# The opening turns of a two-layer graph kernel: loads, weight sums and the first attention in another order

## The chip, the cores and the metric

One core of a Trainium2 chip runs the kernel as a single program. The metric is the device time of one execution in microseconds (us), lower is better; the times given are medians of several executions on the chip. The profile is of one execution more, recorded by the hardware profiler. Its engines are PE (TensorE, matrix products), DVE (VectorE), ACT (ScalarE), POOL (GpSimd) and SP (SyncE, which issues the DMAs here).

## The reference

Two layers are computed on x, 128 graphs of 64 nodes with 768 features. The second layer is ordinary masked attention and is not touched. The first is this, cut to what matters (W has 12 heads of 64 features):

```python
h = jnp.einsum('bnd,ade->bane', feat_in, W)
th = jnp.tanh(h)
attn_src = jnp.einsum('bane,aeo->bano', th, w_src)
attn_dst = jnp.einsum('bane,aeo->bano', th, w_dst)
attn = attn_src + jnp.swapaxes(attn_dst, 2, 3)
attn = jnp.where(attn >= 0, attn, LEAKY_ALPHA * attn)
attn = jnp.where(~adj[:, None, :, :], jnp.float32(-999.0), attn)
attn = jax.nn.softmax(attn, axis=-1)
feat_out = jnp.einsum('banm,bame->bane', attn, h) + b
feat_out = jax.nn.elu(feat_out)          # heads side by side
gate = jax.nn.sigmoid(feat_in @ H_w.T + H_b)
return gate * feat_out + (1.0 - gate) * feat_in
```

Around each layer stand a residual and a layer norm: `x = _layernorm(x + layer(x))`. The second layer begins with v, q and k, products of that x with three more 768 x 768 weights.

## The kernel before

The 8192 rows are cut into 64 tiles of 128 rows (two graphs each), and two tiles make a pair: 32 pairs (`NP`). The first layer's loop (L851) takes a turn for each pair, and one more turn for what is left over.

**Products.** Each 256 x 768 times 768 x 768 product is split into 2 x 2 blocks and done with seven block products instead of eight (Winograd's variant of Strassen's scheme). That needs sums of the blocks of both operands. `block_sums` (L165) makes four sums of x's blocks, and `weight_sums` (L146) four of a weight's blocks, in place:

```python
lambda: eng.tensor_tensor(w[:, T1], w[:, T3], w[:, B11], ALU.subtract),
lambda: eng.tensor_tensor(w[:, T2], w[:, B22], w[:, T1], ALU.subtract),
lambda: eng.tensor_tensor(w[:, T4], w[:, B21], w[:, T2], ALU.subtract),
lambda: eng.tensor_tensor(w[:, T3], w[:, B22], w[:, T3], ALU.subtract),
```

The block of the weight that is loaded as T3 is the upper right one. The seven block products have numbers; number i reads the weight block `OF_B[i]`: 1 reads B11, 2 B21, 3 B22, 4 T4, 5 T1, 6 T2, 7 T3. Products 1, 2, 3 and 4 read x's own blocks or its fourth sum, 5, 6 and 7 its first three sums. A `Job` (L181) is one such product: h (features of all heads, weight w0), g (gate, weight hw) and v (values of the second layer, weight wv). Products 6, 7 and 4 add onto the bank that 1 left. `way_out` (L212) brings a bank out: h on ACT (`S.copy`) for first blocks and on DVE for additions, g wholly on DVE, v like h. `step` (L238) issues a block product and then the way out of the product before it.

**Order.** All instructions are placed by hand (`manual_schedule`): each engine runs its own in the order in which the code issues them, and waits where an input isn't there. `TURN` (L65) lists the 21 products of a turn: "h1" is product 1 of the new pair's h, "g" its gate, "v" the old pair's values, "u" what was left of v's products of the pair before. After the product at position `pos`, everything that `at(pos, ...)` has put into the plan (L871 on) is issued. While the new pair p gets its h and g, the old pair q = p - 1 gets its attention. In the first turn there is no old pair and no v, so the list shrinks to the 14 products of h and g.

**The attention of a tile** goes through these steps, in order: `products` (L633, tanh on ACT, product with the w_dst and w_src rows on DVE and POOL), `terms` (L642, the sums `sd` on DVE, their write to DRAM `dstd` and the read back `dd`), `with_bias` (L659, POOL adds b to h, two DMAs make the half-swapped copy `hx`), `logits` (L671, DVE), `leaky` (L683, ACT), `masked` (L687, DVE), `exps` (L700, ACT, `prob`), `probs_by_nodes` (L718, PE transposes, ACT copies to `pT`), `attend` (L729, 24 small PE products), `features` (L745, DVE, then exp on ACT), `residual` (L763, POOL), `elu1` and `gated` (L768, L773, DVE), `stats` and `normed` (the layer norm), `by_features` (L791, PE transposes of x1, ACT copies to `x1T`), and `v_begins`, which lets v's products start. `mask` (L806) loads a pair's adjacency and makes `nadj` of it on DVE. Tile t1 of a pair comes first, t0 after.

**Opening.** Before the loop (L541 to L557) SP issues, in this order: x transposed of pair 0 (768 KB), four blocks of w0 (576 KB each), four of hw, the two rows of wsd, hb, b0, four blocks of wv. The sums of x are made on POOL, w0's on DVE, then hw's on POOL, then b0 + 1 and wv's four sums on DVE. Only then does the loop begin, so on DVE all of these stand ahead of the first ways out.

Of the kernel before, what the change touches and what calls it, by code (L numbers as in the profile page):

```python
# [49 lines left out]

LAST = [
    "u4", "u3", "q1", "q2", "k1", "k2", "q6", "q5", "q7", "Q1", "q4", "Q2", "q3", "k6", "k5", "k7",
# [10 lines left out]
    "h1", "h2", "u4", "u3", "h6", "g1", "h5", "h7", "g2", "g6", "h4",  # L66
    "h3", "g5", "g7", "v1", "v2", "g4", "v6", "g3", "v5", "v7",
]


@with_exitstack
def kernel(
# [58 lines left out]
        nc.sync.dma_start(out=t, in_=src.rearrange("(f p) -> p f", p=P))  # L131
        return t

    def load_weight(src, tag, name):

        w = wpool.tile([P, 7, HK, HALF], F32, tag=tag, name=name)
        for block in (B11, B21, B22, T3):
            load_block(src, w, block)
        return w

# [5 lines left out]
    def weight_sums(eng, w):  # L146

        return [
# [6 lines that stand above are left out]
    def all_of(steps):  # L155
        for s in steps:
            s()
# [351 lines left out]
    with ExitStack() as ph, ExitStack() as ph_r:  # L509
# [3 lines left out]
        def load_rows(pool, src, n, name):  # L513
            t = pool.tile([P, n], F32, name=name, bufs=1)
            nc.sync.dma_start(out=t, in_=src.partition_broadcast(P))
            return t

        def load_xT(p):
            t = sbr.tile([P, KC, PAIR * P], F32, tag="xT", name=f"xT_{p}")
            nc.sync.dma_start(out=t, in_=xT[p])  # L520
            return t

        def load_x(p):
            ts = []
# [16 lines left out]
        xTs = {0: load_xT(0)}  # L541

        w0_w = weights["q"] = load_weight(w0, "wa", "w0_wq")
        hw_w = weights["k"] = load_weight(hwT, "wb", "hw_wk")
        wsd = sbr.tile([P, 2, D], F32, name="wsd", bufs=1)
        nc.sync.dma_start(out=wsd[:, 0, :], in_=wdst.partition_broadcast(P))
        nc.sync.dma_start(out=wsd[:, 1, :], in_=wsrc.partition_broadcast(P))
        hb_bc = load_rows(sbr, hb, D, "hb_bc")
        b01_bc = load_rows(sb, b0, E0, "b01_bc")
        A = {}  # L550
# [37 lines left out]
        def h_job(p):  # L588
            def at(m, n):
                return h_of(p, m)[:, n * J0 : (n + 1) * J0, :E0]  # L590

            def as_heads(b):
                return b.rearrange("p (j e) -> p j e", e=E0)

            return token_job(
                f"h{p}",
                A[p],
                w0_w,
                lambda mn, b: S.copy(at(*mn), as_heads(b)),
                lambda mn, b: V.tensor_tensor(at(*mn), as_heads(b), at(*mn), ALU.add),  # L600
                lambda b: S.copy(at(1, 0), as_heads(b)),
            )
# [201 lines left out]
            nc.sync.dma_start(out=x1T_d[p], in_=x1Ts[p])  # L804

        def mask(p):  # L806
            ad = load_adj(sb, 2 * p, PAIR, f"adj_{p}")
# [25 lines left out]
            B[q], v_sums[q] = sums_of(V, sb, "sv", x1Ts[q], f"v{q}")  # L833

        def x_sums(p):
            A[p], steps = sums_of(G, sbr, "sx", xTs[p], f"x{p}")
            all_of(steps)

        row_sums = []

# [6 lines left out]
            jobs["q"], jobs["k"] = feature_jobs(0, 0)  # L847
            jobs["Q"], jobs["K"] = feature_jobs(0, 1)

        v_sums = {}  # L850
        for p in range(NP + 1):  # L851
            q = p - 1
            new, old = p < NP, 0 <= q < NP
            t0, t1, n0, n1 = 2 * q, 2 * q + 1, 2 * p, 2 * p + 1
            if new:
                jobs["h"], jobs["g"] = h_job(p), gate_job(p)
            plan = {}

            def at(pos, ok, *acts):
                if ok:  # L860
                    plan.setdefault(pos if new else LAST_AT.get(pos, pos), []).extend(acts)
# [10 lines left out]
            at(1, old, do(residual, t1))  # L872
            at(2, old, do(attend, t1), do(gate_tanh, t0))
            at(3, old, do(features, t1), do(probs_by_nodes, t0), do(residual, t0))
            at(4, old, do(elu1, t1), do(gated, t1))
            at(5, old, do(attend, t0), do(stats, t1))
            at(6, old, do(features, t0), do(normed, t1))
            at(7, old, do(elu1, t0), do(gated, t0))
            at(8, old, do(by_features, t1), do(stats, t0))
            at(9, old, do(normed, t0))  # L880
            at(12, old, do(v_begins))
            at(15, old, lambda: v_sums[q][0](), lambda: v_sums[q][1](), do(spill_features, q))
            at(16, old, lambda: v_sums[q][2]())
            at(19, old, lambda: v_sums[q][3]())

            at(0, p + 1 < NP, lambda: xTs.__setitem__(p + 1, load_xT(p + 1)))
# [4 lines left out]
            at(11, old, do(by_features, t0))  # L891
# [6 lines left out]
            at(17, p + 1 < NP, do(x_sums, p + 1))  # L898
# [21 lines left out]
            for pos, (job, i) in enumerate(TURN if new else LAST):  # L920
                ok = {"h": new, "g": new, "v": old, "u": 0 <= p - 2 < NP}.get(job, True)
                if ok:
                    step(jobs[job], int(i))
                else:
                    flush()
# [115 lines left out]
```

## Time and profile before

| | us |
|---|---|
| median of 3 runs | 2976.0 (2974.97 to 2976.16) |
| the profiled execution | 2976.17 |
| its span in the profile | 2974.4 |
| PE busy | 2921.3 |
| DVE, ACT, POOL busy | 1819.8, 1006.3, 821.0 |

The span runs from the first to the last recorded instruction. In a row of the timeline the columns are the start, the duration, the engine, the line of the kernel, the operation, what it writes and reads (buffer numbers left out), how many records are merged, and in brackets the idle time of that engine before it with what ended it. A block product of h, g or v appears as six matmul records. The granted clock of PE (PEclk) is 1.00 at full speed.

The time of PE by stretch of the opening (busy us of 7.60, 21.06 and so on; further columns left out here):

| stretch, us | PE busy | DVE busy | POOL busy | PEclk |
|---|---|---|---|---|
| 0 to 8.88 | 0.00 | 0.15 | 2.18 | 1.00 |
| 8.88 to 16.48 | 6.10 | 2.83 | 2.41 | 1.00 |
| 16.48 to 37.54 | 9.91 | 9.76 | 10.52 | 0.82 |
| 37.54 to 64.13 | 19.00 | 14.42 | 11.97 | 0.82 |
| 64.13 to 79.56 | 11.85 | 11.53 | 3.69 | 0.78 |
| 79.56 to 142.94 | 63.38 | 49.66 | 20.60 | 1.00 |

### The profile page before, as it was taken

What the parts mean: (1) busy time and instruction counts of PE and PEld (TensorE: products, weight loads), DVE (VectorE), ACT (ScalarE), POOL (GpSimd) and SP (SyncE); (2) the same over time, 40 slices, a digit from 0 to 9 for tenths busy, and PEclk for the clock granted to TensorE, in tenths of its full rate; (3) what the DMA queues carried; (4) which work ended last, traced back from release to release, by engine and by line L of the source; (5) the groups of instructions that cost most, each with busy time, mean ns of one, the idle gap of its engine ahead of it and who ended that gap; (6) DMA issues with size and microseconds to landing.
All of it is one profiled execution on the core that took longest, in us unless ns stands there. A gap on an engine that the chain in (4) does not pass through costs nothing.

```text
span 2974.4 us, 45312 instructions
## 1 busy us (share of the span) xinstructions
PE 2921.3 (98%) x18048; PEld 2021.3 (68%) x18048; DVE 1819.8 (61%) x3013; ACT 1006.3 (34%) x1761; POOL 821.0 (28%) x654
## 2 busy tenths in 40 slices
PE   5999999999999999999989999999999999999999
PEld 3666666666666666666578777787777887777875
DVE  4888888888888888888844334433443443443345
ACT  2444444443444444434422222222222222222221
POOL 4333333243233333433422211212111212121121
PEclk8999999999999999999999999999999999999999
DMA  5334333333333333333523211222112222112221
GB/s 171 100 111 128 102 118 117 114 108 110 119 120 102 118 126 105 110 113 121 175 88 92 69 58 57 86 86 76 63 54 67 86 76 72 58 56 83 87 80 48
DMA packets 179537, 284.81 MB, mean 96 GB/s; under 512 B 46720, under 2 KB 113280, under 8 KB 179328
## 3 DMA queue, kind: packets, MB, share of 16 engines
q1 hardware_dynamic: 179328, 281.93, 29.1%
q8 instruction: 143, 2.34, 0.3%
q14 instruction: 66, 0.54, 0.1%
HBM read 167.81 MB, written 101.06 MB: 90 GB/s over the span
## 4 chain that ended last, share of the span: by engine, by line
PE 95%; DVE 2%; DMA 2%; SPq 1%; ACT 0%; issue 0%; POOL 0%; POOLq 0%; DVEq 0%; ACTq 0%
PE y_o L203 8%; PE y_k L203 8%; PE y_h L203 8%; PE y_v L203 8%; PE y_g L203 8%; PE y_q L203 8%; PE z_h L203 4%; PE z_v L203 4%; PE z_o L203 4%; PE z_k L203 4%; PE z_q L203 4%; PE z_g L203 4%; PE x_o L203 2%; PE x_k L203 2%; PE x_v L203 2%; PE x_g L203 2%
## 5 line engine op out<-in xcount | busy, mean ns | idle before, releaser
L766 POOL TENSOR_TENSOR x<-gate,x 128x768 f32<-128x768 f32 x64 | 117.2, 1831 | 315.3 <-ACT gate L817 315.3
L438 POOL TENSOR_TENSOR y<-y,bf_bc 128x768 f32<-128x768 f32 x64 | 115.8, 1839 | 308.7 <-DMA y<-x1d 308.7
L462 DVE TENSOR_TENSOR y<-y_o,y 128x384 f32<-128x384 f32 x128 | 71.3, 557 | 202.2 <-PE y_o L203 199.4
L320 DVE TENSOR_TENSOR kT<-z_k,kT 128x256 f32<-128x256 f32 x96 | 40.7, 424 | 238.6 <-PE z_k L203 135.3
L639 POOL TENSOR_TENSOR th<-th,wsd 128x768 f32<-128x768 f32 x64 | 116.3, 1817 | 159.5 <-DVE th L638 159.5
L255 POOL TENSOR_TENSOR rs_b<-ve_b,minus_half 128x1 f32<-128x1 f32 x64 | 35.2, 549 | 453.2 <-DVE ve_b L253 451.3
L173 POOL TENSOR_TENSOR sq_q<-a,a 128x768 f32<-128x768 f32 x16 | 29.7, 1855 | 432.8 <-PE y_o L203 315.9
L203 PE MATMUL y_g<-hw_wk,sx_x 128*128 128x384 f32 x384 | 136.5, 492 | 11.1 <-DVE gate L615 11.1
L203 PE MATMUL y_h<-w_wq,xT 128*128 128x384 f32 x384 | 137.4, 495 | 8.9 <-DMA w_wq<-in_w_dram 8.9
L203 PE MATMUL y_k<-a,hw_wk 128*128 128x256 f32 x576 | 144.6, 387 | 0.0
L203 PE MATMUL y_q<-a,w_wq 128*128 128x256 f32 x576 | 140.2, 379 | 1.5 <-ACT qT L319 1.5
L203 PE MATMUL y_q<-sq_q,w_wq 128*128 128x256 f32 x576 | 140.3, 380 | 1.4 <-ACT qT L319 1.2
L203 PE MATMUL y_k<-sq_q,hw_wk 128*128 128x256 f32 x576 | 140.1, 379 | 1.4 <-ACT kT L319 1.4
L255 POOL TENSOR_TENSOR rs_a<-ve_a,minus_half 128x1 f32<-128x1 f32 x64 | 35.3, 552 | 382.6 <-DVE ve_a L253 382.6
L203 PE MATMUL z_q<-sq_q,w_wq 128*128 128x256 f32 x576 | 140.1, 379 | 0.0
L203 PE MATMUL z_k<-sq_q,hw_wk 128*128 128x256 f32 x576 | 140.0, 379 | 0.0
L203 PE MATMUL z_v<-wv,sv_v 128*128 128x384 f32 x384 | 137.5, 494 | 1.6 <-DVE v L629 1.6
L319 ACT ACTIVATE qT<-y_q,bq_c 128x256 f32<-128x256 f32 x144 | 67.4, 469 | 211.8 <-PE y_q L203 211.8
L203 PE MATMUL y_v<-wv,sv_v 128*128 128x384 f32 x384 | 136.6, 492 | 1.5 <-DVE sv_v L174 1.5
L367 ACT ACTIVATE sc<-sc 128x512 f32<-128x512 f32 x48 | 30.2, 630 | 318.5 <-DVE sc L366 318.5
L203 PE MATMUL z_h<-w_wq,sx_x 128*128 128x384 f32 x384 | 137.5, 494 | 0.0
L203 PE MATMUL y_h<-w_wq,sx_x 128*128 128x384 f32 x384 | 136.0, 491 | 1.5 <-DVE w_wq L150 1.5
(167 smaller groups left out, 6807.5 us busy)
## 6 DMA issues: line engine op xcount, KB each, us to landing
xT<-in_xT_dram SPq DMA_DIRECT2D x32, 768.0 KB, 6.7
x<-in_x_dram SPq DMA_DIRECT2D x64, 384.0 KB, 3.6
dd<-dstd SPq DMA_DIRECT2D x128, 192.0 KB, 3.4
x1d<-x SPq DMA_DIRECT2D x64, 384.0 KB, 2.5
x1Td<-x1T SPq DMA_DIRECT2D x32, 768.0 KB, 4.8
vd<-v SPq DMA_DIRECT2D x64, 384.0 KB, 2.9
a<-x1Td SPq DMA_DIRECT2D x64, 384.0 KB, 3.6
v<-vd SPq DMA_DIRECT2D x384, 64.0 KB, 2.3
```

The lines of the kernel that those rows point to most:

```text
L173: lambda: e.tensor_tensor(s1, a21, a22, ALU.add),
L203: T.matmul(to[:, : self.n], lhsT, rhs, start=kc == 0 and not more, stop=kc == HK - 1, skip_group_check=more,)
L255: G.tensor_tensor(rstd, ve, minus_half, ALU.pow)
L319: lambda mn, bk_: S.activation(at(*mn), bk_, AF.Identity, bias=bias(mn[1])),
L320: lambda mn, bk_: V.tensor_tensor(at(*mn), bk_, at(*mn), ALU.add),
L367: S.activation(sc, sc, AF.Exp, scale=SCALE)
L438: G.tensor_tensor(y, y, pools["bf"], ALU.add)
L462: V.tensor_tensor(at(*mn), b, at(*mn), ALU.add)
L639: G.tensor_tensor(th[:, 1, :], th[:, 1, :], wsd[:, 1, :], ALU.mult)
L766: G.tensor_tensor(xp, st[t]["gate"], xp, ALU.mult)
```

## The change

The first three turns get lists and places of their own, and the rest of the loop keeps `TURN`.

- **Loads.** x transposed of pair 0 comes in two halves, each ahead of the w0 blocks that need it; w0's T3 ahead of its B22; hb and b0 ahead of hw; hw in the order B11, B21, T3, B22; wsd after hw; wv's blocks are issued inside the first turn, after pair 0's x.
- **Weight sums.** w0's on DVE in the order T1, T2, T3, T4. hw's on DVE (POOL before), one each after positions 6 to 9 of the first turn. wv's on DVE after positions 4, 5, 7 and 8 of the second turn. b0 + 1 after position 7 of the first.
- **First turn** (`FIRST`, 13 products): h mostly ahead of the gate; g4 goes into the second turn as "G4". Pair 1's sums of x come at position 12.
- **Second turn** (`SECOND`, 22 products): pair 1's h and g, G4, then "H1" (the next pair's h1), v1, v2, v6, v5, v7 of pair 0 and "H2". The new pair's steps and the old pair's steps have separate tables of places, so that pair 0's attention begins at position 6 or later. Steps placed past the end of a list are carried into the next turn.
- **Third turn**: `TURN` without its first two products, and all steps two positions earlier.
- **All turns**: the adjacency's load stays at position 3, `nadj` on DVE moves from position 3 to 6.

```diff
+FIRST = ["h1", "h2", "h5", "h6", "g1", "h7", "g2", "h4", "g6", "g5", "g7", "h3", "g3"]
+FIRST_AT = {3: 0, 6: 10, 8: 3, 11: 8, 12: 12, 13: 12, 14: 13, 15: 14, 16: 14, 17: 14, 18: 15, 19: 16, 20: 17}
+SECOND = [
+    "h1", "G4", "h2", "g1", "g2", "h6", "h5", "h7", "g6", "h4",
+    "g5", "g7", "h3", "g4", "g3", "H1", "v1", "v2", "v6", "v5", "v7", "H2",
+]
+SECOND_AT = {11: 10, 12: 13, 13: 13, 14: 14, 15: 14, 16: 15, 17: 16, 18: 18, 19: 19, 20: 20}
+SECOND_OLD = {
+    0: 7, 1: 7, 2: 8, 3: 9, 4: 10, 5: 11, 6: 12, 7: 12, 8: 13, 9: 14, 11: 15, 12: 15, 15: 16, 16: 17, 19: 19,
+}
+THIRD_AT = {pos: max(pos - 2, 0) for pos in range(len(TURN))}
+TURNS = {
+    0: (FIRST, FIRST_AT, {}),
+    1: (SECOND, SECOND_AT, SECOND_OLD),
+    2: (TURN[2:], THIRD_AT, THIRD_AT),
+}
...
-        w0_w = weights["q"] = load_weight(w0, "wa", "w0_wq")
-        hw_w = weights["k"] = load_weight(hwT, "wb", "hw_wk")
+        for kh, blocks in ((0, (B11,)), (1, (B21, T3, B22))):
+            rows = slice(kh * HK, (kh + 1) * HK)
+            nc.sync.dma_start(out=xTs[0][:, rows, :], in_=xT[0][:, rows, :])
+            for block in blocks:
+                load_block(w0, w0_w, block)
+        hb_bc = load_rows(sbr, hb, D, "hb_bc")
+        b01_bc = load_rows(sb, b0, E0, "b01_bc")
+        hw_w = weights["k"] = load_weight(hwT, "wb", "hw_wk", (B11, B21, T3, B22))
...
-        all_of(weight_sums(V, w0_w))
-        all_of(weight_sums(G, hw_w))
-        V.tensor_scalar(b01_bc, b01_bc, 1.0, None, ALU.add)
-        wv_w = load_weight(wv, "wc", "wv")
-        all_of(weight_sums(V, wv_w))
+        t1, t2, t4, t3 = weight_sums(V, w0_w)
+        all_of((t1, t2, t3, t4))
+        wv_w = wpool.tile([P, 7, HK, HALF], F32, tag="wc", name="wv")
...
-            at(0, old, do(probs_by_nodes, t1), do(exps, t0), do(gate_tanh, t1))
+            was(0, do(probs_by_nodes, t1))
+            at(0, old, do(exps, t0), do(gate_tanh, t1), places={0: 6} if p == 1 else of_old)
...
-            at(3, new, do(mask, p))
+            at(3, new, lambda: adjs.__setitem__(p, load_adj(sb, 2 * p, PAIR, f"adj_{p}")))
+            at(6, new, do(mask, p))
...
+            at(17, p + 1 < NP, do(x_sums, p + 1), places={17: 12} if p == 0 else of_new)
...
+            if p == 0:
+                for pos, act in zip((6, 7, 8, 9), weight_sums(V, hw_w)):
+                    at(pos, True, act, places={})
+                for block in (B11, B21, T3, B22):
+                    at(8, True, do(load_block, wv, wv_w, block))
+                at(7, True, lambda: V.tensor_scalar(b01_bc, b01_bc, 1.0, None, ALU.add))
+            if p == 1:
+                at(14, True, third_begins, places={})
+                for pos, act in zip((4, 5, 7, 8), weight_sums(V, wv_w)):
+                    at(pos, True, act, places={})
+            for pos, acts in carried.items():
+                plan[pos] = acts + plan.get(pos, [])
+            carried = {pos - len(turn): acts for pos, acts in plan.items() if pos >= len(turn)}
+            for pos, (job, i) in enumerate(turn):
+                step(jobs[job], int(i))
```

`third_begins` prepares H, pair 2's h, from the two of x's blocks that its products 1 and 2 read; its sums of x come in the third turn. `was` is `at` for the old pair's steps with their own table of places.

More of the change, by code (lines that the diff above doesn't have):

```diff
@@ L132, in load_cols, with load_weight @@
         return t
-    def load_weight(src, tag, name):
+    def load_weight(src, tag, name, order=(B11, B21, B22, T3)):
         w = wpool.tile([P, 7, HK, HALF], F32, tag=tag, name=name)
-        for block in (B11, B21, B22, T3):
+        for block in order:
             load_block(src, w, block)
@@ L520, in load_xT @@
             nc.sync.dma_start(out=t, in_=xT[p])
-            return t
+            xTs[p] = t
         def load_x(p):
@@ L539, in sums_of @@
             )
-        xTs = {0: load_xT(0)}
-        w0_w = weights["q"] = load_weight(w0, "wa", "w0_wq")
-        hw_w = weights["k"] = load_weight(hwT, "wb", "hw_wk")
+        xTs, A = {}, {}
+        xTs[0] = sbr.tile([P, KC, PAIR * P], F32, tag="xT", name="xT_0")
+        w0_w = weights["q"] = wpool.tile([P, 7, HK, HALF], F32, tag="wa", name="w0_wq")
+        for kh, blocks in ((0, (B11,)), (1, (B21, T3, B22))):
[6 more added lines that the diff above has]
+        hw_w = weights["k"] = load_weight(hwT, "wb", "hw_wk", (B11, B21, T3, B22))
         wsd = sbr.tile([P, 2, D], F32, name="wsd", bufs=1)
@@ L547 @@
         nc.sync.dma_start(out=wsd[:, 1, :], in_=wsrc.partition_broadcast(P))
-        hb_bc = load_rows(sbr, hb, D, "hb_bc")
-        b01_bc = load_rows(sb, b0, E0, "b01_bc")
-        A = {}
         A[0], x_steps = sums_of(G, sbr, "sx", xTs[0], "x0")
         all_of(x_steps)
-        all_of(weight_sums(V, w0_w))
-        all_of(weight_sums(G, hw_w))
-        V.tensor_scalar(b01_bc, b01_bc, 1.0, None, ALU.add)
-        wv_w = load_weight(wv, "wc", "wv")
-        all_of(weight_sums(V, wv_w))
+        t1, t2, t4, t3 = weight_sums(V, w0_w)
+        all_of((t1, t2, t3, t4))
+        wv_w = wpool.tile([P, 7, HK, HALF], F32, tag="wc", name="wv")
         def work(name):
@@ L806, in mask @@
         def mask(p):
-            ad = load_adj(sb, 2 * p, PAIR, f"adj_{p}")
+            ad = adjs.pop(p)
             na = sb.tile([P, PAIR, N], U8, tag="nadj", name=f"nadj_{p}", bufs=2)
@@ L835, in x_sums, with third_begins @@
         def x_sums(p):
-            A[p], steps = sums_of(G, sbr, "sx", xTs[p], f"x{p}")
+            operands, steps = sums_of(G, sbr, "sx", xTs[p], f"x{p}")
             all_of(steps)
+            A.setdefault(p, {}).update(operands)
+        def third_begins():
+            x = xTs[2]
+            A[2] = {1: x[:, :HK, :P], 2: x[:, HK:, :P]}
+            jobs["H"] = h_job(2)
         row_sums = []
@@ L848, in queries_begin @@
             jobs["Q"], jobs["K"] = feature_jobs(0, 1)
-        v_sums = {}
+        v_sums, carried = {}, {}
         for p in range(NP + 1):
@@ L855, with at, was @@
             if new:
-                jobs["h"], jobs["g"] = h_job(p), gate_job(p)
+                jobs["G"] = jobs.get("g")
+                jobs["h"], jobs["g"] = jobs["H"] if p == 2 else h_job(p), gate_job(p)
             plan = {}
-            def at(pos, ok, *acts):
+            turn, of_new, of_old = TURNS.get(p, (TURN, {}, {})) if new else (LAST, {}, LAST_AT)
+            def at(pos, ok, *acts, places=of_new):
                 if ok:
-                    plan.setdefault(pos if new else LAST_AT.get(pos, pos), []).extend(acts)
+                    plan.setdefault(places.get(pos, pos), []).extend(acts)
+            def was(pos, *acts):
+                at(pos, old, *acts, places=of_old)
             def do(f, *args):
@@ L868, in v_begins @@
                 jobs["v"] = v_job(q)
-            at(0, old, do(probs_by_nodes, t1), do(exps, t0), do(gate_tanh, t1))
[L872 to L886, printed above, removed]
-            at(3, new, do(mask, p))
+            was(0, do(probs_by_nodes, t1))
+            at(0, old, do(exps, t0), do(gate_tanh, t1), places={0: 6} if p == 1 else of_old)
+            was(1, do(residual, t1))
+            was(2, do(attend, t1), do(gate_tanh, t0))
+            was(3, do(features, t1), do(probs_by_nodes, t0), do(residual, t0))
+            was(4, do(elu1, t1), do(gated, t1))
+            was(5, do(attend, t0), do(stats, t1))
+            was(6, do(features, t0), do(normed, t1))
+            was(7, do(elu1, t0), do(gated, t0))
+            was(8, do(by_features, t1), do(stats, t0))
+            was(9, do(normed, t0))
+            was(12, do(v_begins))
+            was(15, lambda: v_sums[q][0](), lambda: v_sums[q][1](), do(spill_features, q))
+            was(16, lambda: v_sums[q][2]())
+            was(19, lambda: v_sums[q][3]())
+            at(0, p + 1 < NP, do(load_xT, p + 1))
+            at(3, new, lambda: adjs.__setitem__(p, load_adj(sb, 2 * p, PAIR, f"adj_{p}")))
+            at(6, new, do(mask, p))
             at(4, 0 <= p - 2 < NP, do(spill_values, p - 2))
@@ L890 @@
             at(11, new, do(products, n1))
-            at(11, old, do(by_features, t0))
+            was(11, do(by_features, t0))
             at(12, new, do(products, n0))
@@ L897 @@
             at(17, new, do(leaky, n1))
-            at(17, p + 1 < NP, do(x_sums, p + 1))
+            at(17, p + 1 < NP, do(x_sums, p + 1), places={17: 12} if p == 0 else of_new)
             at(18, new, do(masked, n1), do(logits, n0))
@@ L919 @@
                     plan.setdefault(pos, []).append(act)
[L920 to L925, printed above, removed]
+            if p == 0:
[13 more added lines that the diff above has]
+                step(jobs[job], int(i))
                 for act in plan.get(pos, ()):
```

## The prediction

> **What bounds the kernel now.** I read the page's busy table first, then its slices, then the granted clock and busy time by window, then TensorE's own timeline with its waits, and last the timeline of the other engines inside each gap. Times are of the profiled execution (span 2974.4 us, 2976.17 us by its own clock, 0.2 us above the median 2976.0), so differences in span carry over to the median one to one.
>
> ```profile
> PE 2921.3 (98%) x18048; PEld 2021.3 (68%) x18048; DVE 1819.8 (61%) x3013; ACT 1006.3 (34%) x1761; POOL 821.0 (28%) x654
> PE   5999999999999999999989999999999999999999
> PEclk8999999999999999999999999999999999999999
> ```
>
> TensorE is busy 98% of the span, and the change alters no product. Only idle time (53.1 us in all, 2974.4 - 2921.3) and half-clock time can be won. The slices put the loss in the first one (74 us). TensorE's timeline, cut to the stalls:
>
> ```profile
> 8.88 4.16 PE L203 MATMUL y_h<-w_wq,xT 128*128 128x384 f32 x6 [8.88 <-DMA w_wq<-in_w_dram]
> 12.85 2.13 PE L203 MATMUL x_h<-w_wq,xT 128*128 128x384 f32 x6
> 16.48 2.17 PE L203 MATMUL y_h<-w_wq,sx_x 128*128 128x384 f32 x6 [1.50 <-DVE w_wq L150]
> 37.54 4.18 PE L203 MATMUL y_g<-hw_wk,sx_x 128*128 128x384 f32 x6 [11.15 <-DVE gate L615]
> 51.95 2.20 PE L203 MATMUL y_g<-hw_wk,xT 128*128 128x384 f32 x6 [1.49 <-DVE gate L615]
> 64.13 1.54 PE L715 MATMUL pTp<-ident,prob 128*128 128x128 f32 x6 [6.11 <-ACT prob L704]
> 72.86 0.52 PE L715 MATMUL pTp<-ident,prob 128*128 128x128 f32 x3 [3.41 <-DVE rden L752]
> ```
>
> The bracket is the idle time before the row and what ended it. A product (6 records) starts 1.94 us after the one before it at full clock and lasts about 3.9 at half clock, as in the first and fourth rows. Up to 79.56, where TensorE becomes dense and stays so, it did 18 products (34.8 us), 12 transposes (1.3) and one attend (0.9): 37.0 us of work in 79.6. So 42.6 us are lost: 32.7 idle (8.88+1.50+11.15+1.49+6.11+3.41+0.17) and about 9.9 of half clock. That is the most the change can win, less the load that cannot go.
>
> Why the 11.15 us: VectorE had these in front of its drains of TensorE's banks:
>
> ```profile
> 30.91 1.36 DVE L149 TENSOR_TENSOR wv<-wv 128x1152 f32<-128x1152 f32 x1 [5.63 <-DMA wv<-in_wv_dram]
> 34.98 1.35 DVE L152 TENSOR_TENSOR wv<-wv 128x1152 f32<-128x1152 f32 x1
> 36.84 0.55 DVE L615 TENSOR_TENSOR gate<-y_g,hb_bc 128x384 f32<-128x384 f32 x1
> 57.65 1.54 DVE L675 TENSOR_TENSOR att<-dd,sd 128x768 f32<-128x768 f32 x1 [3.51 <-DMA dd<-dstd]
> ```
>
> The gate's first drain stands behind the four sums of wv, which wait for wv's load. The last row starts pair 0's attention, which has to be over before VectorE's next drains.
>
> **What the Trainium skill says.** "TensorE: Matmul & The Clock Gate", section "What's actually happening": the clock halves after an idle window of about 3.4 us and is restored after a busy one, on free-running windows. The trace agrees: PEclk is 0.50 at 30 to 42 us, after the 11.15 us gap, and again at 62 to 66. "SBUF — State Buffer", section "Two separate sides": a VectorE operation with two SBUF inputs and a GpSimd operation exclude each other for a whole instruction. The trace agrees that they delay each other: `nadj` (L809) takes 218 ns at least and 1700 at the median, the sum L151 of w_wq has two instances with a mean of 2155 ns, the first (16.36 us, POOL idle) at 1.36, so the other, in the stage where POOL also makes weight sums, at 2.95. "Perfetto Trace Analysis", section "Per-engine timelines": ACT and VectorE are strict FIFOs, so an early wait holds all behind it. The 11.15 us gap is that.
>
> **The change part by part.** I date each step of the new order with the durations above and those of the same rows of before: every instruction starts at the later of its engine being free and its last input being there. The same arithmetic on the old order puts pair 1's first v product at 143.4, against 142.94 in the trace. All "after" dates are estimates made so.
>
> *Loads.* While loading, DMA moves 372 to 392 GB/s (windows of 2 us, 8 to 20 us). Before, h1 needed 768 KB of xT and 576 KB of w0, 1.38 MB, and started at 8.88. Now it needs 384 + 576 KB, 0.98 MB: about 1.0 us earlier, 7.9. It runs cold as before. T3 lands ahead of B22, so w0's first sum ends near 14.0, and h5, which needs only it, goes at 14.2 instead of h6 at 16.48. hb and b0 (0.43 MB, 1.1 us) now precede hw, whose first block is there near 17, before g1 at 18.1. wv goes behind x and lands near 35; its first sum is near 61. SP has issued it by 25, so pair 0's small transfers (from 43) do not queue behind it. One more issue of 0.5 us on SP is hidden: the transfers are behind the issues (w0 issued by 5.3, landed at 13.6).
>
> *hw's sums, from POOL to VectorE, between drains.* Four of 2.61 us on POOL (to 30.5) become four of 1.36. Order of the gate after h: g6 waits 0.6 for the second sum (26.5). The third (28.6) meets POOL's th product (1.82 us, L639 before) in the shared port and costs about 2.7; then a drain and the fourth: g7 waits 2.8 until 33.2. The 11.15 us stall has become 3.4.
>
> *h ahead of the gate.* h3 at 36.8 completes h, tanh (0.84), th product (0.96) and sums (1.74 each, L646) follow, and the small write goes out at 42.9 instead of 51.45. Write, read back and logits took 6.2 us before (51.45 to 57.65): att at 49.2, 8.5 us earlier.
>
> *Attention over pair 1's products.* TensorE has h1, g4, h2, g1, g2, h6, h5 of the second turn, from 40.7 to 54.2, where it idled before. Then it follows the attention chain, which is now VectorE's without a gap from 49 to 90: the chain of before plus four sums of wv (4 x 1.36, more beside POOL's L766), plus pair 1's drains. Stalls: 3.8 at 54.2 (h7 needs ACT's copy of h6, which stands in ACT's FIFO behind the leaky of t0, and that waits for VectorE's logits), 1.1 (h4), 1.6 (transposes of t0), 1.4 and 3.5 (transposes of x1, the second at 89.6), 1.2 (v1), about 2.2 in small ones after. The 3.8 and the 3.5 each straddle a window, so about 5 us of half clock come with them, beside 1.7 to 3.4 at the start.
>
> *Sum.* Idle after: 7.9 + 0.6 + 2.8 + 3.8 + 1.1 + 1.6 + 1.4 + 3.5 + 1.2 + 2.2 = 26.1; half clock about 7.5; together 33.6 against 42.6: 9.0 us won. By dates: pair 1's first v product at 134.2 against 142.94, 8.7. All work up to there is the same, and after it TensorE is dense to 1472 in before, so the gain stays.
>
> *Edits priced at nothing.* `nadj` moves from position 3 to 6 in every turn and leaves POOL's L766: up to 1.5 us of VectorE in each of 31 turns, worth 0, as no TensorE wait between 80 and 1472 us would see it. On POOL, pair 1's sums of x (4 x 0.99) move ahead of t0's bias on h, which comes 4 us later relative to the chain; hx of t0 is read by attend t0 some 20 us after. The third turn: h1 and h2 of pair 2 move forward with their loads (x transposed lands about 54, used at 84).
>
> **Unknown costs.** The phase of the clock windows moves the gain between 7.5 and 10.5 by the same dates. Each sum of hw or wv costs 1.36 to 2.95; I took the low end unless POOL stands beside it: -2 to +6 us. The ACT stall of 3.8 is 0 if the logits of t0 come 4 us sooner, 6 if the port holds them.
>
> **Rivals.**
> *A, forecast:* turn 1 follows VectorE's chain, 9 us won: 2976 - 9 = 2967, own range 2962 to 2971.
> *B, the gaps close further:* if the 2.8, 3.8 and 3.5 stalls with their half clock (5) stay mostly out, 10 more: about 2957. For it: each of the three hangs on one instruction's place in a FIFO, and a chain that runs 3 us faster than dated (no meeting in the port, quicker read back) frees all. Against: VectorE has no idle time to give between 49 and 90.
> *C, no change:* two of the three gaps are worse by 3 us and bring a window each: 2974.
> *D, slower:* wv's sums in the attention chain. Before they ran beside an idle POOL; now all four could lie beside POOL's products (2.95 instead of 1.36: 6.4 us), and a chain that long idles TensorE into two or three more half-clock windows (1.7 each, 5): 11.4 against 9 won gives 2978, with TensorE cold again a few us more: 2979. It decides from 9 us of added chain. Against: POOL has only two products (3.6 us) near them.
> *E, not what it says:* the loads land in the new order too late, since SP's issue waits for earlier transfers (hw's four blocks took 5.07 us to issue, w0's four 2.34). Then g1 waits for hw; hw's bytes are 1.1 us behind before, and g1 has 1 us of slack, so worth 1 us at most, inside A.
>
> **How the numbers follow.** A 0.58, B 0.22, C 0.13, D 0.07. What can be told from no change is about 0.2%, 6 us. Faster is B and nearly all of A: 0.79; same 0.14; slower 0.07. Predicted 2967. The range reaches into B and C: 2957 to 2973.
>
> **What would show it.** TensorE's timeline: first product near 7.9, no gap over 4 us after it, dense from about 92; the dstd write near 43; the wv sums after 60, at 1.4 us where POOL is idle; the third sum of hw near 2.7. Wrong: a first gap over 5 us before 40, VectorE idle for long between 49 and 90 while TensorE waits, or any new wait after 150.

## The result, and the profile after

The changed kernel takes 2967.9 us (median of 13 runs, 2965.4 to 2970.9) against 2976.0 for the kernel before in the same session (13 runs, 2974.3 to 2976.8): ratio 0.9975, 95% interval 0.9966 to 0.9983, 8.1 us won. The forecast was 2967. The profiled execution is one of the slower ones (2970.8 us, span 2969.0), so its late part loses more than the median does.

The page after: busy times, then TensorE's busy tenths and granted clock in 40 slices.

```profile
PE 2925.2 (99%) x18048; PEld 2023.0 (68%) x18048; DVE 1796.9 (61%) x3017; ACT 1009.0 (34%) x1761; POOL 811.1 (27%) x650
PE   7999999999999999999999999999999999999999
PEclk9999999999999999999999999999999999999999
```

It is mainly the first slice that changed (5 to 7 tenths, clock 8 to 9). TensorE's timeline after, cut to its waits and the two landmarks that I use below:

```profile
7.90 3.98 PE L222 MATMUL y_h<-w_wq,xT 128*128 128x384 f32 x6 [7.90 <-DMA w_wq<-in_w_dram]
33.11 2.20 PE L222 MATMUL y_g<-hw_wk,sx_x 128*128 128x384 f32 x6 [2.16 <-DVE hw_wk L171]
56.89 4.18 PE L222 MATMUL y_h<-w_wq,sx_x 128*128 128x384 f32 x6 [4.17 <-ACT h L622]
80.39 0.87 PE L738 MATMUL x1Tp<-ident,x 128*128 128x128 f32 x6 [1.17 <-ACT x L278]
88.44 0.87 PE L738 MATMUL x1Tp<-ident,x 128*128 128x128 f32 x6 [3.31 <-ACT x L278]
90.27 3.78 PE L222 MATMUL y_v<-wv,x1T 128*128 128x384 f32 x6 [0.95 <-ACT x1T L739]
133.39 2.10 PE L222 MATMUL y_v<-wv,x1T 128*128 128x384 f32 x6
139.98 2.17 PE L222 MATMUL y_v<-wv,sv_v 128*128 128x384 f32 x6 [0.62 <-DVE sv_v L193]
```

The 11.15 us gap has become 2.16. The 6.11 ahead of the transposes of the probabilities is gone, and 4.17 stands at pair 1's seventh product of h instead. The row at 133.39 is pair 1's first v product, which started at 142.94 before: 9.55 us earlier. The other landmark is SP's first write of `dstd`, with which the chain of the attention of pair 0 begins, 41.40 against 51.45 before. SP's row of the changed kernel, then the two landmarks of the kernel before, from SP's and TensorE's timelines:

```profile
41.40 0.34 SPq L671 DMA_DIRECT2D dstd<-sd  x1
```

```profile
51.45 0.33 SPq L648 DMA_DIRECT2D dstd<-sd  x1
...
142.94 2.10 PE L203 MATMUL y_v<-wv,x1T 128*128 128x384 f32 x6
```

VectorE of the changed kernel around it: the last sum of hw, the logits that wait for the read back, and the first sum of wv.

```profile
30.56 2.50 DVE L171 TENSOR_TENSOR hw_wk<-hw_wk 128x1152 f32<-128x1152 f32 x1
47.54 2.59 DVE L698 TENSOR_TENSOR att<-dd,sd 128x768 f32<-128x768 f32 x1 [4.04 <-DMA dd<-dstd]
59.38 1.35 DVE L168 TENSOR_TENSOR wv<-wv 128x1152 f32<-128x1152 f32 x1
```

So the dates of the prediction that these lines show hold within 1.7 us. Whether its reasons do is what the experiments ask.

### The profile page after: what moved, and what is told of

It is laid out like the page before. It is cut to its first block, busy times and chain, and to the rows that moved or that the text cites. A ratio compares the mean times of both kernels' runs of the same rounds, so it can differ in the third digit from the quotient of the medians.

```text
span 2969.0 us, 45314 instructions
## 1 busy us (share of the span) xinstructions
PE 2925.2 (99%) x18048; PEld 2023.0 (68%) x18048; DVE 1796.9 (61%) x3017; ACT 1009.0 (34%) x1761; POOL 811.1 (27%) x650
## 4 chain that ended last, share of the span: by engine, by line
PE 94%; DVE 3%; DMA 1%; ACT 1%; issue 0%; SPq 0%; POOLq 0%; POOL 0%; DVEq 0%; ACTq 0%
PE y_k L222 8%; PE y_o L222 8%; PE y_q L222 8%; PE y_v L222 8%; PE y_h L222 8%; PE y_g L222 8%; PE z_v L222 4%; PE z_o L222 4%; PE z_k L222 4%; PE z_h L222 4%; PE z_q L222 4%; PE z_g L222 4%; PE x_k L222 2%; PE x_o L222 2%; PE x_q L222 2%; PE x_h L222 2%
## 5 line engine op out<-in xcount | busy, mean ns | idle before, releaser
L222 PE MATMUL y_v<-wv,x1T 128*128 128x384 f32 x384 | 136.1, 491 | 1.2 <-ACT x1T L739 1.0
```

What stands on the lines that cost most here:

```text
L222: T.matmul(to[:, : self.n], lhsT, rhs, start=kc == 0 and not more, stop=kc == HK - 1, skip_group_check=more,)
```

## The experiments

All eleven in one table; "v" is the start of pair 1's first v product, "dstd" that of the first `dstd` write, both in the profile. The ratio is to the kernel before in the same session (its median there 2975.3 to 2976.0).

| kernel | median us | ratio, 95% interval | dstd | v | v - dstd |
|---|---|---|---|---|---|
| before | 2976.0 | 1 | 51.45 | 142.94 | 91.5 |
| changed | 2967.9 | 0.9975, 0.9966 to 0.9983 | 41.40 | 133.39 | 92.0 |
| e1 sums only | 2976.7 | 1.0005, 0.9997 to 1.0013 | 48.35 | 143.30 | 95.0 |
| e2 no spread | 2966.7 | 0.9969, 0.9958 to 0.9981 | 41.66 | 132.40 | 90.7 |
| e3 nadj only | 2975.6 | 1.0001, 0.9993 to 1.0009 | 49.90 | 143.28 | 93.4 |
| e4 loads back | 2967.3 | 0.9973, 0.9964 to 0.9982 | 41.65 | 133.41 | 91.8 |
| e5 sums and mask | 2965.9 | 0.9966, 0.9954 to 0.9979 | 38.82 | 133.81 | 95.0 |
| e6 adj early | 2961.4 | 0.9950, 0.9938 to 0.9963 | 37.19 | 128.77 | 91.6 |
| e7 no wv sums | 2967.1 | 0.9969, 0.9958 to 0.9980 | 42.83 | 133.34 | 90.5 |
| e8 ACT free | 2970.5 | 0.9985, 0.9978 to 0.9991 | 41.47 | 134.12 | 92.7 |
| e9 h first | 2957.5 | 0.9940, 0.9928 to 0.9953 | 33.45 | 125.73 | 92.3 |
| e10 spread by one | 2964.6 | 0.9963, 0.9950 to 0.9975 | 37.10 | 131.67 | 94.6 |
| e11 h late | 2967.0 | 0.9971, 0.9960 to 0.9982 | 42.94 | 134.72 | 91.8 |

**e1: the weight sums alone.** The kernel before with hw's and wv's sums moved as the change moves them.

```diff
-        all_of(weight_sums(G, hw_w))
-        V.tensor_scalar(b01_bc, b01_bc, 1.0, None, ALU.add)
...
-        all_of(weight_sums(V, wv_w))
...
+            if p == 0:
+                for pos, act in zip((5, 6, 8, 9), weight_sums(V, hw_w)):
+                    at(pos, True, act)
+                at(7, True, lambda: V.tensor_scalar(b01_bc, b01_bc, 1.0, None, ALU.add))
+            if p == 1:
+                for pos, act in zip((4, 5, 7, 8), weight_sums(V, wv_w)):
+                    at(pos, True, act)
```

> The kernel before with part (b) alone: hw's four sums on VectorE inside turn 0 (after products h5, h7, g2 and g6), b0+1 beside them, wv's four sums inside turn 1; loads, order of the products and attention as before. Theory S (the weight sums carry the whole gain; the reordered products and the spread attention only trade one wait of TensorE for others): pair 1's first v product starts near 134 (estimate from the rows of before: 11.15 us of waiting for the seventh product of the gate go, the wait of 7.3 us ahead of the transposes of the probabilities stays, and later waits of some 2 us come with wv's sums), and the time is 8 to 9 us under before, as the whole change. Theory P (the parts add, as the prediction has it: sums about half, the attention spread over pair 1 the other half): landmark 138 to 139, 4 to 5 us under before.

Neither theory: nothing is won. TensorE still waits 9.52 us for the gate's sixth product; TensorE's, VectorE's and SP's timelines of e1:

```profile
36.03 3.60 PE L203 MATMUL y_g<-hw_wk,sx_x 128*128 128x384 f32 x6 [9.52 <-DVE hw_wk L150]
```

```profile
32.74 0.23 DVE L806 TENSOR_SCALAR nadj<-adj 128x128 uint8<-128x128 uint8 x1 [13.17 <-DMA adj<-in_adj_dram]
32.89 1.35 DVE L149 TENSOR_TENSOR hw_wk<-hw_wk 128x1152 f32<-128x1152 f32 x1
```

```profile
15.20 5.10 SPq L144 DMA_DIRECT2D wv<-in_wv_dram  x4
...
21.90 0.72 SPq L263 DMA_DIRECT2D adj<-in_adj_dram  x1
```

VectorE stands 13.17 us at `nadj`, which stands at position 3 and reads the adjacency. The load of 16 KB was issued at 21.90, behind wv's four blocks, and came in at 32.7. The sums of hw are queued behind it. The kernel before has the same load behind the same blocks, but there it doesn't show: wv's sums held VectorE until 36.3, and `nadj` ran at 36.71 with no idle time before it:

```profile
36.71 0.22 DVE L809 TENSOR_SCALAR nadj<-adj 128x128 uint8<-128x128 uint8 x1
```

**e2: no spread.** The changed kernel with pair 0's attention at the end of the first turn, and `TURN` for the second and third.

```diff
-FIRST = ["h1", "h2", "h5", "h6", "g1", "h7", "g2", "h4", "g6", "g5", "g7", "h3", "g3"]
-FIRST_AT = {3: 0, 6: 10, 8: 3, 11: 8, 12: 12, 13: 12, 14: 13, 15: 14, 16: 14, 17: 14, 18: 15, 19: 16, 20: 17}
+FIRST = ["h1", "h2", "h5", "h6", "g1", "h7", "g2", "h4", "g6", "g5", "g7", "h3", "g4", "g3"]
+FIRST_AT = {3: 0, 6: 10, 8: 3, 11: 8, 12: 12, 13: 12, 14: 13, 15: 13, 16: 13, 17: 13, 18: 13, 19: 13, 20: 13}
...
-    1: (SECOND, SECOND_AT, SECOND_OLD),
-    2: (TURN[2:], THIRD_AT, THIRD_AT),
+    1: (TURN[:2] + TURN[4:], THIRD_AT, THIRD_AT),
```

> The changed kernel with its loads and sums and with h ahead of the gate in turn 0, but without the spread: pair 0's masks, maxima and exponentials stand at the end of turn 0, turn 1 keeps the old list of products from its start, and no product of a turn is issued in the turn ahead of it or after it. Theory S: one wait of about 12 us ahead of the first transposes of the probabilities near 57 us, few waits after it, pair 1's first v product near 134.7, time within 1 us of the changed kernel. Theory P: the waits of 4.17, 0.67, 1.17 and 3.31 us of the spread version add up to less than the 12 us wait, so this one loses 3 to 5 us against the changed kernel (landmark 137 to 139).

TensorE's wait ahead of the transposes of the probabilities in e2:

```profile
53.79 1.54 PE L737 MATMUL pTp<-ident,prob 128*128 128x128 f32 x6 [10.48 <-ACT prob L726]
```

One long wait of 10.48 us, and v starts 1.0 us earlier than in the changed kernel and 2.3 earlier than theory S had it. The intervals of the two ratios overlap: the spread is worth nothing that can be measured. Theory S is right on this, P is not.

**e3: `nadj` alone**, in the kernel before, position 3 to 6 in every turn.

```diff
-            at(3, new, do(mask, p))
+            at(3, new, lambda: adjs.__setitem__(p, load_adj(sb, 2 * p, PAIR, f"adj_{p}")))
+            at(6, new, do(mask, p))
```

> The kernel before with one edit: the comparison that makes nadj moves from position 3 to position 6 of every turn, its load stays at 3. Prediction's step: 0, landmark 143, time within 0.5 us of before. Rival: the mask's wait for its load held VectorE's queue somewhere, so that all turns gain or lose, over 1 us in the sum of the turns.

0.4 us slower in the median, no difference. The gap stays (10.82), and in the other 31 turns the move gives nothing.

**e4: the old loads** in the changed kernel.

```diff
-        for kh, blocks in ((0, (B11,)), (1, (B21, T3, B22))):
...
+        load_xT(0)
+        w0_w = weights["q"] = load_weight(w0, "wa", "w0_wq")
+        hw_w = weights["k"] = load_weight(hwT, "wb", "hw_wk")
...
+        wv_w = load_weight(wv, "wc", "wv")
```

> The changed kernel with the loads of the kernel before (xT in one piece, w0 and hw in the order B11, B21, B22, T3, the bias rows after the rows of wdst and wsrc, wv straight after them). Prediction's step: the first product starts near 9.0 instead of 7.9 and about 1 us is lost (landmark 134.4), or 1.5 if the gate's sixth product then waits longer. Rival E (early loads are hidden anyway by VectorE's chain that turn 1 follows): the late start is absorbed by the 4.17 us wait near 54 us, and the time is within 0.4 us of the changed kernel.

TensorE's timeline of e4, first product, third product, and the seventh of the gate:

```profile
8.70 3.86 PE L222 MATMUL y_h<-w_wq,xT 128*128 128x384 f32 x6 [8.70 <-DMA w_wq<-in_w_dram]
14.92 2.17 PE L222 MATMUL z_h<-w_wq,sx_x 128*128 128x384 f32 x6 [0.42 <-DVE w_wq L168]
...
33.36 2.20 PE L222 MATMUL y_g<-hw_wk,sx_x 128*128 128x384 f32 x6 [2.17 <-DVE hw_wk L171]
```

The start is 0.80 us later, the third product 0.25 (14.92 against 14.67), v 0.02. Rival E is right: the order of the loads is worth nothing in this kernel. With `nadj` behind hw's sums, adj's late landing doesn't hold them either.

**e5: e1 and one more edit.** In the first turn `nadj` stands at position 10, behind hw's sums.

```diff
-            at(3, new, do(mask, p))
+            at(3 if p == 0 else 3, new, lambda: adjs.__setitem__(p, load_adj(sb, 2 * p, PAIR, f"adj_{p}")))
+            at(10 if p == 0 else 3, new, do(mask, p))
```

> The kernel of e1 (weight sums on VectorE alone) with one more edit: in turn 0 nadj's comparison stands at position 10 instead of 3, behind hw's sums; the load of adj and all else stay. Theory Q (e1 gained nothing because VectorE's queue stood for 13.17 us at nadj, whose 16 KB load had come in only at 32.7 us behind wv's four blocks, so hw's sums started at 32.89 instead of near 20): the wait ahead of the gate's sixth product falls from 9.52 to about 0.5 to 2 us, pair 1's first v product starts at 133 to 135 against 143.30, and the time is 8 to 10 us under before, where each of the two edits alone gave nothing (e1 and e3). Rival R (VectorE is full anyway and the sums delay the attention by what they win): landmark 140 to 143, at most 3 us under before.

Theory Q: 9.7 us under before, as much as the whole change gives. The sums alone gave nothing (e1), and neither did moving `nadj` alone, though e3 moved it to position 6 of every turn and not to 10 of the first. VectorE's and TensorE's timelines of e5:

```profile
27.39 1.35 DVE L152 TENSOR_TENSOR hw_wk<-hw_wk 128x1152 f32<-128x1152 f32 x1
33.32 0.23 DVE L806 TENSOR_SCALAR nadj<-adj 128x128 uint8<-128x128 uint8 x1 [4.12 <-DMA adj<-in_adj_dram]
```

```profile
39.31 3.85 PE L203 MATMUL y_g<-hw_wk,xT 128*128 128x384 f32 x6 [3.07 <-DVE gate L612]
```

The late load still costs: `nadj` now waits 4.12, and so the steps queued behind it come later, among them the drain of the gate for which TensorE waits 3.07.

**e6: adj's load ahead of wv's**, and the changed kernel's order of loads.

```diff
+                for block in (B11, B21, T3, B22):
+                    at(4, True, do(load_block, wv, wv_w, block))
...
-                for pos, act in zip((4, 5, 7, 8), weight_sums(V, wv_w)):
+                for pos, act in zip((0, 5, 9, 10), weight_sums(V, wv_w)):
```

> A version meant to beat both: e5 with the order of loads of the changed kernel, adj's load ahead of wv's (which is issued from position 4 of turn 0), and wv's first sum at position 0 of turn 1, in VectorE's wait for dstd, the others at positions 5, 9 and 10; no h ahead, no spread. Theory Q: landmark near 128 to 130 (estimate: the wait at the gate's fourth product falls to about 1.8 us, the 7.3 us ahead of the first transposes of the probabilities stay, the sum of wv in the dstd wait is free), and 3 to 5 us under the changed kernel. Rival P (h ahead and the spread are worth their own share): landmark 134 to 138, not under the changed kernel.

14.2 us under before, 6.5 below the changed kernel's median where 3 to 5 were expected. The wait at the gate's fourth product is 1.48. v - dstd falls from 95.0 to 91.6. Whether the new places of wv's sums have a part in that is not shown: where those places alone changed it did not fall (e11 91.8, e2 90.7).

**e7: no sums of wv**, in the changed kernel.

```diff
-                for pos, act in zip((4, 5, 7, 8), weight_sums(V, wv_w)):
-                    at(pos, True, act, places={})
```

> The changed kernel without wv's four weight sums (left out; the three blocks that they would fill are set to zero near the start). They took 5.4 us of VectorE between 59 and 68. Theory V (TensorE follows VectorE's chain from 47 to 90 us): the start of pair 0's first v product moves from 90.27 to 85 to 86.5, landmark 128 to 130, 4 to 5 us gained. Rival F (each stall of TensorE has its own cause in ACT's or VectorE's queue, and the sums lie beside it): the two waits of 4.17 and 3.31 stay and under 1.5 us is gained, landmark 132 to 133.5.

The kernel leaves the sums out, and the three blocks that they would fill hold zeros (three memsets near the start, not in the cut above), so v is not the layer's. Rival F. The same window of the changed kernel and then of e7 (stretch, its length, then busy us of PE, weight loads, DVE, ACT and POOL with their instructions, clock, DMA share, GB/s):

```profile
60.00:90.00 30.00, 23.08 (x170) 13.68 (x168) 26.52 (x41) 13.99 (x22) 12.03 (x9) 0.95 0.15 43
```

```profile
60.00:90.00 30.00, 24.84 (x172) 15.10 (x171) 21.26 (x38) 14.19 (x21) 11.54 (x9) 0.90 0.15 42
```

VectorE has 5.3 us less to do, and TensorE's two waits for x1 are the same to 0.01 us:

```profile
58.32 4.18 PE L222 MATMUL y_h<-w_wq,sx_x 128*128 128x384 f32 x6 [4.17 <-ACT h L624]
...
80.63 0.87 PE L740 MATMUL x1Tp<-ident,x 128*128 128x128 f32 x6 [1.16 <-ACT x L278]
88.69 1.54 PE L740 MATMUL x1Tp<-ident,x 128*128 128x128 f32 x6 [3.31 <-ACT x L278]
```

The chain began 1.43 us later (dstd 42.83, mostly because a product of the gate fell into half clock), and v started at the same time: the four sums cost some 1.5 us in these two profiles, not 5.4. So it isn't VectorE's throughput that TensorE follows there but a chain of dependent steps, each with its own wait, beside which the sums mostly fit.

**e8: ACT's queue freed** ahead of the 4.17 us wait: exp and leaky issued after the copy of h6.

```diff
-FIRST_AT = {3: 0, 6: 10, 8: 3, 11: 8, 12: 12, 13: 12, 14: 13, 15: 14, 16: 14, 17: 14, 18: 15, 19: 16, 20: 17}
+FIRST_AT = {3: 0, 6: 10, 8: 3, 11: 8, 12: 12, 13: 12, 14: 13, 15: 14, 16: 14, 17: 14, 18: 15, 19: 19, 20: 20}
...
-                for pos, act in zip((4, 5, 7, 8), weight_sums(V, wv_w)):
+                for pos, act in zip((7, 8, 8, 9), weight_sums(V, wv_w)):
```

> The changed kernel with pair 0's exp of tile 1 and leaky of tile 0 issued after the copy of h's sixth product (positions 16 and 17 of turn 0's list become 19 and 20, three more positions into turn 1), wv's sums moved to positions 7, 8, 8, 9 so that they stay behind the masks. Rival F: the 4.17 us wait of h's seventh product goes and with it the half clock after it, 4 to 7 us gained, landmark 127 to 130. Theory V: the wait only moves to the next product that needs VectorE's chain (the fourth product of h near 65 us waits some 5 us), landmark 133 to 136, nothing gained or up to 2 us lost.

Theory V. The wait is gone and back two products later, in e8's timeline of TensorE:

```profile
63.25 3.90 PE L222 MATMUL y_h<-w_wq,xT 128*128 128x384 f32 x6 [3.59 <-ACT h L622]
70.13 1.57 PE L738 MATMUL pTp<-ident,prob 128*128 128x128 f32 x6 [2.98 <-DVE rden L775]
```

v starts 0.7 us later, and the median is 2.6 above the changed kernel's; the intervals of the two ratios overlap, so a loss is not shown, but neither is any gain. Two of wv's sums met POOL here (2.23 and 2.85 us in place of 1.35).

**e9: h ahead of all but two of the gate's products**, on e6. hw's sums, wv's loads and pair 0's steps move forward with it.

```diff
+FIRST = ['h1', 'h2', 'h5', 'h6', 'g1', 'h7', 'g2', 'h4', 'h3', 'g6', 'g5', 'g7', 'g4', 'g3']
...
-                for pos, act in zip((5, 6, 8, 9), weight_sums(V, hw_w)):
+                for pos, act in zip((4, 5, 6, 7), weight_sums(V, hw_w)):
```

> The version of e6 with all of h's products ahead in turn 0: h1 h2 h5 h6 g1 h7 g2 h4 h3 g6 g5 g7 g4 g3, so that h's last product h3 is the 9th product (10th in the kernel before and in e6, 12th in the changed kernel); hw's sums follow products 5 to 8, the actions on pair 0's tiles one product after the h that they need. Theory H (in turn 0 the place of h's last product dates the chain of the attention, and the changed kernel put it later, not earlier): dstd is written near 32 to 34 us (37.19 in e6, 41.40 in the changed kernel), the wait ahead of the first transposes shrinks below 5 us, pair 1's first v product starts at 124 to 126 and 2 to 4 us are gained against e6. Rival: VectorE or the loads of hw hold the chain, landmark 128 or later, nothing gained against e6.

Theory H. SP's and TensorE's timelines of e9:

```profile
33.45 0.33 SPq L652 DMA_DIRECT2D dstd<-sd  x1
```

```profile
42.29 3.11 PE L206 MATMUL z_g<-hw_wk,sx_x 128*128 128x384 f32 x6 [4.21 <-DVE gate L620]
54.93 1.57 PE L719 MATMUL pTp<-ident,prob 128*128 128x128 f32 x6 [3.35 <-DVE rden L756]
```

dstd 3.7 us earlier than in e6, v 3.0 earlier, and 2957.5 us: 17.8 under before, the fastest kernel of the study. The wait ahead of the first transposes is gone; VectorE's drain of the gate now makes one of 4.21.

**e10: e6 with the attention spread by one product.** Every step of pair 0 in the second turn up to `x1`'s transposes one product later, the v products where they were. The list of the turn leaves out the two u, so `o` maps the old positions to the new ones.

```diff
-            at(0, old, do(probs_by_nodes, t1), do(exps, t0), do(gate_tanh, t1))
+            at(o(0), old, do(probs_by_nodes, t1), do(exps, t0), do(gate_tanh, t1))
...
+SECOND_OLD = {0: 1, 1: 2, 2: 2, 3: 2, 4: 3, 5: 4, 6: 5, 7: 6, 8: 7, 9: 8, 10: 9, 11: 10, 12: 10, 13: 11, 14: 12, 15: 13, 16: 14, 17: 15, 18: 16, 19: 17, 20: 18}
```

> The version of e6 with the attention of pair 0 spread a little over pair 1: every action of pair 0 in turn 1 (transposes, attention, features, normalization, transposes of x1) one product later, the v products where they were. Theory W (each return of the chain to TensorE now queues behind one more product of 1.94 us, so a spread lengthens the chain by more than the first wait shrinks): the first wait falls by about 2 us, later waits of 3 to 6 us come ahead of the v products, landmark 130 to 133 against 128.77, 1.5 to 4 us lost against e6. Theory P (the prediction's: filling the first wait is a gain): landmark 126.5 to 127.5, 1 to 2 us gained.

wv's last three sums move by one product too. Theory W. TensorE's wait ahead of the first transposes in e6, then TensorE's timeline of e10:

```profile
49.97 1.54 PE L716 MATMUL pTp<-ident,prob 128*128 128x128 f32 x6 [6.22 <-ACT prob L705]
```

```profile
49.81 1.04 PE L720 MATMUL pTp<-ident,prob 128*128 128x128 f32 x6 [4.21 <-ACT prob L709]
...
85.52 2.20 PE L207 MATMUL y_g<-hw_wk,xT 128*128 128x384 f32 x6 [1.44 <-DVE gate L620]
90.32 3.19 PE L207 MATMUL y_v<-wv,sv_v 128*128 128x384 f32 x6 [2.60 <-DVE sv_v L178]
```

The first wait fell from 6.22 to 4.21, and 1.44 and 2.60 stand at 85 and 90; v starts 2.9 us later than in e6, and the median is 3.1 higher.

**e11: e2 with wv's sums where e6 has them.**

```diff
-                for pos, act in zip((4, 5, 7, 8), weight_sums(V, wv_w)):
+                for pos, act in zip((0, 3, 7, 8), weight_sums(V, wv_w)):
```

> e2 (the changed kernel's loads, sums and order of turn 0, no spread) with wv's sums at the places of e6 (the first behind turn 1's first product, in the wait for dstd; the others at products 4, 8 and 9). It differs from e6 mainly by turn 0's order of products, with h3 12th instead of 10th. Theory H: the order keeps its loss, landmark 131.5 to 133, 3 to 4 us slower than e6. Rival (the places of wv's sums made e6 faster than e2): landmark 128 to 129.5, within 1 us of e6.

Theory H, with 2 us more loss than written: 5.6 us slower than e6, v 5.95 later, dstd 5.75 later. The expected 131.5 to 133 was missed by 1.7. Against e2, whose program is the same up to there, dstd is 1.3 later, after a product of the gate that began to run at half clock:

```profile
32.95 3.35 PE L221 MATMUL y_g<-hw_wk,sx_x 128*128 128x384 f32 x6 [2.16 <-DVE hw_wk L170]
```

## Why the prediction was right, and where its reasons were not

The time, the sign and the dates came out (v forecast at 134.2, measured 133.4). They came out because the working dated the changed order as a whole; what each part is worth alone did not enter. The reading of the cause did not come out, and the table shows it: in all thirteen kernels v starts 90.5 to 95.0 us after the first `dstd` write. The spread, built to shorten that stretch, left it at 92.0 against 91.5. The 9.55 us won at v go with the date of `dstd`, 10.05 us earlier. No run moves that date alone, and the stretch is constant only within those 4.5 us: in e1 `dstd` came 3.1 earlier and v did not. Luck has a share too: the phase of the clock moves `dstd` by some 1.3 us (last section).

*The first gap.* The prediction laid the 11.15 us to wv's sums ahead of the gate's drains. That was the wait that ended last, but another stood right behind it in the same queue. e1 took wv's sums out and hw's off POOL and gained nothing. **The step that failed is "`nadj` ... worth 0"**: it holds for the other turns (e3), but in the first turn `nadj` moves behind hw's sums, and with that edit the move of the sums counts (e5: 9.7 us, where e1 gave none). I priced `nadj` by the steady turns alone and gave the first turn's own place (`6: 10`) no line.

*Loads.* Said to win about 1.0 us at the start. The start came 0.98 us earlier than in the kernel before and 0.80 earlier than in e4, and nothing of it was left at v (e4). Rival E bounded it rightly at 1 us.

*hw's sums on VectorE.* Right in kind: g7 waits 2.16 us where 2.8 was said. The sum that met POOL was the fourth (2.50 us), not the third; 2.7 was said.

*"h ahead of the gate", 8.5 us for `dstd`.* `dstd` came 10.05 us earlier, but not for that reason. The list does not put h ahead: in `FIRST` h's last product is the 12th; in the old list, without the products that the first turn lacks, it is the 10th. With the gap gone the old order writes `dstd` at 37.19 (e6), the changed one at 41.40, and the one with h's last product 9th at 33.45 (e9). By these dates the reorder costs about 4 us, and 5.6 in the medians of e6 and e11: of the 14.2 us that e6 wins, the changed kernel keeps 8.1.

*Attention over pair 1's products.* The prediction counted the 6.11 us wait as won and named the stalls that come instead: 3.8 at 54.2 was 4.17 at 52.7, the 3.5 that was to end at 89.6 was 3.31 and ended at 88.4. Its sum of these stalls was nearly right, and trading the one wait for them gains nothing (e2; in e10 it loses 3.1). The statement that TensorE follows "VectorE's without a gap" is wrong: without 5.4 us of VectorE's work the waits stay (e7). What fits the runs is that TensorE follows the latency of the attention's steps: each return of that chain to TensorE stands behind the product in progress, so a spread over more products lengthens it, as e10 was expected to show and did. The single stalls aren't causes either: the one with ACT's queue moved away leaves and returns two products later (e8). Rival B rested on freeing them.

*Half clock.* Said 7.5 us. The clock column reads 1.00 over the first two products (8 to 12 us), so there only their length tells: they took 14.67 - 0.85 - 7.90 = 5.9 us where two take 3.9 at full clock: 2.0 lost. The windows after them are these (columns as above):

```profile
56.00:62.00 6.00, 5.11 (x12) 3.22 (x13) 5.93 (x7) 3.17 (x6) 0.00 (x0) 0.50 0.02 5
62.00:64.00 2.00, 2.00 (x7) 1.25 (x6) 2.00 (x2) 0.85 (x3) 1.92 (x1) 0.81 0.01 4
64.00:90.00 26.00, 19.08 (x158) 11.07 (x156) 22.52 (x38) 11.17 (x17) 10.11 (x9) 1.00 0.18 50
90.00:94.00 4.00, 3.73 (x7) 2.16 (x8) 1.30 (x1) 0.98 (x3) 3.92 (x6) 0.57 0.72 226
```

Busy time by one minus clock gives 2.6, 0.4, 0 and 1.6, so some 6.6 in all. One reading of the prediction needs a correction: the 0.50 from 30 us on is not after the 11.15 us gap, which ran from 26.39 to 37.54, but begins some 3.6 us into it.

*Rival D, sums of wv in the chain.* They ran at 1.34 to 1.35 each, away from POOL. That they would cost 5 to 11 us is refuted from the other side by e7; e8, where two met POOL, is the nearest to D.

*"The gain stays."* Not quite. 9.55 us at v are 8.1 in the median. From v to the same product 29 turns later the four kernels with the shortened third turn (changed, e4, e7, e8) take 1323.4 to 1323.6 us, and the other nine 1322.4 to 1322.7: the shortened third turn costs 0.9, of which 0.62 is the wait at 139.98 in the first timeline. The rest is scattered: where the first layer ends, the wait of z_v for VectorE was 1.5 to 3.2 us in the thirteen profiles, with and without the shortened turn. Why it varies isn't settled. It wasn't tried to undo the third turn alone.

*Signs and readings.* Two signs did not come: "no gap over 4 us" (4.17), and hw's third sum near 2.7 (1.35; it was the fourth that was slow). Two of the readings are loose. The loads' windows of 8 to 20 us show 370 to 392 GB/s, not 372. And of the two operations that it sets beside the rule on two SBUF inputs, only the weight sum has two; `nadj` reads one tensor, so its 1.70 us beside POOL is a measurement of its own.

## What to carry to other kernels

A wait has one releaser in the profile, but its queue can hold several. Before pricing the removal of one, ask of every instruction behind it when its own input lands; small loads issued behind large ones are the first suspects. And price a chain by the date of its first link: find the event after which the distance to the end hardly changes (here the `dstd` write, within 4.5 us), and judge a reorder first by what it does to that date, not by the waits that it fills. Edits that give nothing alone can give everything together, so tests that do one part alone need the pair as well.

## What the runs showed of the hardware that was not expected

The same wait can cost a product at half clock or not. The gate's seventh product waits 2.16 us in the changed kernel, e2, e8, e7 and e11, whose programs are the same up to there but for three early memsets in e7. It took 2.20 us in the first three and 3.44 and 3.35 in the last two, and `dstd` is then some 1.3 us later. The section "What's actually happening" of the Trainium skill's "TensorE: Matmul & The Clock Gate" has the windows run free of the program; these five profiles agree with it. So two kernels that differ by 1 us in one profile each can't be told apart by it.
